# Three block products in place of four at a second level of a Toeplitz convolution, with its tables from difference vectors

## The chip, the cores and the metric

The kernel runs on one core of one Trainium2 chip, as one launch. The metric is device time in microseconds, the median of several executions. Five engines run queues of their own: TensorE (PE, with its weight loads as PEld), VectorE (DVE), ScalarE (ACT), GpSimd (POOL) and SyncE (SP), which here only issues DMAs.

## The reference

For x of 2048 tokens by 1024 channels the result is `x + S4(xn) + FFN(xn)`, with xn the layer norm of x. The part that matters here is S4, a causal convolution along the 1024 channels:

```python
K = _s4_kernel(Lambda, p, q, B, Ct, step, L).astype(u.dtype)     # 1024 taps, made from small vectors
y = jnp.fft.irfft(jnp.fft.rfft(u, n=n) * jnp.fft.rfft(K, n=n), n=n)[..., :L]
return y + D[0] * u
```

The FFN multiplies xn with int4 weights (1024 to 2752, gate and up), forms `silu(g) * u` and multiplies with a third int4 matrix (2752 to 1024).

## The kernel before, in words

All matrix work is on PE. A float32 operand is split in two fp16 parts, high and low, and a product is three matmul passes (`PASS`: high by high, high by low, low by high). Token and channel blocks are combined by Strassen-like sums, so that seven products stand for eight.

There are two phases. In the first, to about 844 us, PE multiplies xn by the gate and up weights, 21 groups (`gate_up`) for each of two token halves `cp`. DVE, ACT and POOL dequantize weights meanwhile, and the S4 kernel vector is worked out in small steps (`s4`) between them. The instructions of DVE, ACT, PE and SP are pinned to the order in which they are written there (`pin`). The last gate-up group writes its result in fp16 parts to a DRAM tensor `HPL`, by DMAs on ACT's queue (`last_h`).

The second phase starts with the convolution, from 846.6 to 966.4 us, and ends with the down projection (`operands`, `matmuls`, `evacuate`): 49 products of 60 matmuls of 256 columns each, whose results are added to `out` through DMAs. In this phase a scheduler that keeps its own cost estimates orders each engine's queue when the kernel is built; SBUF tiles come from rotating pools. A pool's first tiles take memory that tiles of the first phase held, and wait for their last readers. A DMA of SP or ACT adds to one of eight counters in turn when it lands, and waits for the DMA that used the counter before.

The convolution as a matrix is a lower triangular Toeplitz matrix of 8 by 8 blocks of 128 channels. A tile of the stage is 128 tokens (`q`, four of them) of one token quarter (`cp`, `c`) by 512 output channels (`hh`: 0 the left half, 1 the right). There are 32 such tiles.

- `band` holds the Toeplitz rows for lags 0 to 1023 in both fp16 parts. It is read from the vector `KP` in DRAM, which the S4 steps wrote, by four overlapping-row DMAs on SP.
- `conv` multiplies four 128-channel blocks of xn (as weights) with 512, 384, 256 and 128 columns of `band`: the triangle. For `hh = 1` it adds the square part, from the other half's four blocks, as a 2 by 2 product of 256-wide blocks with three products for four: two of them with the tables `diff[0]` and `diff[1]`, 256 columns each, in `conv`, and one with the sums `xs` of input blocks, in `last_tiles`, which goes to a bank of its own (`pc`) and is added to both 256-wide halves of the result.
- `diff` comes from `band` by DVE and ACT (`add_split`), `xs` from xn in the same way, eight blocks of 512 tokens.
- `last_tiles` also adds the remaining 192 channels of the down projection, five 512-column matmuls with `wp` (loaded by two DMA transposes of `WPN`) and `hpl` (loaded from `HPL` on ACT's queue). It then loads a tile of x (`p`), adds the PSUM result to it on DVE and stores it to `out`.
- One quarter of the transposed xn is not kept in SBUF and is loaded from `XSP` for each `cp` (x7; in the trace `x<-XSP`).

The order is (c, hh) = (0,0), (0,1), (1,1), (1,0) in the first half, where `last_tiles` runs four tiles behind `conv`, and (0,1), (0,0), (1,1), (1,0) in the second, where it follows at once and the first four operands of the down projection are prepared (`prepare`: loads `a`, `b`, splits `g`). PSUM has eight banks. In the trace, `cv` is a tile's bank, `cc` the bank `pc`, and L77 and L82 are two lines of the wrapper through which engines are called, with and without a pinned order.

Of the kernel before, what the change touches and what calls it, by code (L numbers as in the profile page):

```python
# [24 lines left out]
F16 = mybir.dt.float16  # L25
# [4 lines left out]
ALU = mybir.AluOpType  # L30
# [3 lines left out]
P = 128  # L34
# [21 lines left out]
KS = 64.0  # L56
# [31 lines left out]
def build(nc, tc, x, xp, raw_d, sz_d, par_d, vct_d, tab_d, csrow_d, out):  # L88
# [3 lines left out]
    with es:  # L92
        pool = lambda name, **k: es.enter_context(tc.tile_pool(name=name, **k))
        dr = pool("dr", bufs=1, space=DRAM)
        cst = pool("cst", bufs=1)
# [18 lines left out]
        V, A = Engine(tc, nc.vector), Engine(tc, nc.scalar)  # L114
        SP, G, PE = Engine(tc, nc.sync), nc.gpsimd, Engine(tc, nc.tensor)
# [7 lines left out]
        ident = cst.tile([P, P], F32, name="ident")  # L123
# [11 lines left out]
        home, szbufs = {"nat": weights("right", "nat", bufs=4)}, [4]  # L135
# [10 lines left out]
        xf = {}  # L146
# [141 lines left out]
        with ea:  # L288
# [273 lines left out]
            PASS = ((0, 0), (0, 1), (1, 0))  # L562
# [177 lines left out]
            sm, wx, cf, tmp = s4p[:, 0:32], s4p[:, 32:36], s4p[:, 36:44], s4p[:, 44:46]  # L740
# [66 lines left out]
            def s4_kernel():  # L807
# [4 lines left out]
                M, AD, SB = ALU.mult, ALU.add, ALU.subtract  # L812
# [40 lines left out]
                tab, z, tab2 = tab[:, 0:512], tab[:, 512:896], tab2[:, 0:272]  # L853
                SP.dma_start(tab, tab_d[0])
                SP.dma_start(tab2[0:8], tab_d[1, 0:8, 0:272])
                yield "bank"
                py = bank("s4y")

# [1 line left out]
                    PE.matmul(py[0:8, 0:256], W(8), tab[:, 0:256], start=True, stop=False)  # L860
                PE.matmul(py[0:8, 0:256], W(9), tab[:, 256:512], start=False, stop=True)
                yield "read"
                tc_, ts_ = tab2[0:8, 0:128], tab2[0:8, 128:256]
                yr, yi = py[0:8, 0:128], py[0:8, 128:256]
                zt = z[0:8, 256:384]
# [7 lines left out]
                pk = bank("s4k")[0:8, 0:128]  # L873
                with tc.issue_after(ends[0].ins):
                    PE.matmul(pk, tab2[0:8, 256:264], z[0:8, 0:128], start=True, stop=False)
                PE.matmul(pk, tab2[0:8, 264:272], z[0:8, 128:256], start=False, stop=True)
                yield "read"
                k = z[:, 256:384]
                V.tensor_copy(k[0:8], pk)
                V.scalar_tensor_tensor(k[0:1, 0:1], sm[0:1, 24:25], KS, k[0:1, 0:1], M, AD)  # L880
                kh = cst.tile([8, 2, P], F16, tag="s4kh", name="s4kh")
                split(kh, k[0:8])
# [303 lines left out]
        for b in range(2):  # L1186
            for n in range(2):
                p0 = 64 * b + 32 * n
                base = KP[:, 128 - 64 * b - 62 - n :]
                src = bass.AP(base.tensor, base.offset, [[2, 32], [base.ap[0][0], 2], [1, 1024]])  # L1190
                SP.dma_start(band[p0 : p0 + 32], src)

        def add_split(dst, srcs, op):

            (h0, l0), (h1, l1) = srcs
            n = dst.shape[2]
            t = htile("t")[:, 0:n]
            V.tensor_tensor(t, h0, h1, op)
            V.tensor_tensor(t, t, l0, ALU.add)
            V.tensor_tensor(t, t, l1, op)  # L1200
            A.copy(dst[:, 0], t)
            V.tensor_tensor(dst[:, 1], t, dst[:, 0], ALU.subtract)


        diff = []
        for a0, b0 in ((128, 384), (640, 384)):
            a, b = ([band[:, i, c : c + 384] for i in range(2)] for c in (a0, b0))
            diff.append(htile(f"diff{a0}").bitcast(F16).rearrange("p (a b) -> p a b", a=2)[:, :, 0:384])
            add_split(diff[-1], (a, b), ALU.subtract)
        wp = []  # L1210
        for i in range(2):
            wp.append(bep.tile([P, 2, 1024], F16, tag="be", name=f"wp{i}"))
            SP.dma_start_transpose(wp[i].rearrange("p b (c d) -> p (b c) d", d=P), WPN[:, i])

        def conv(cp, c, hh, q, xc):

            ts = slice(q * P, (q + 1) * P)
            ps = bank(f"cv{cp}{c}{hh}{q}")
            first = [True]

            def mm(dst, w, m):
                PE.matmul(dst, w, m, start=first[0], stop=False, skip_group_check=True)
                first[0] = False

            xt = xc[2 * c + hh]
            for k in range(4):
                for xi, bi in PASS:
                    mm(ps[:, P * k : 512], xt[:, xi, k, ts], band[:, bi, 0 : 512 - P * k])
            if hh:

                xt = xc[2 * c]
                for k in range(2):
                    for xi, bi in PASS:
                        mm(ps[:, 0:256], xt[:, xi, k + 2, ts], diff[0][:, bi, P - P * k : P - P * k + 256])
# [5 lines left out]
        def last_tiles(ps, cp, c, hh, q, hpl, xs):  # L1240

            ts = slice(q * P, (q + 1) * P)
            cols = slice(512 * hh, 512 * hh + 512)
            mm = lambda w, m, stop=False: PE.matmul(ps, w, m, start=False, stop=stop, skip_group_check=True)
            for hi, wi in PASS:
# [6 lines left out]
            V.scalar_tensor_tensor(o, ps, osc, o, ALU.mult, ALU.add)  # L1252
            if hh:
                pc = bank(f"cc{cp}{c}{q}")
                for k in range(2):
                    for n, (xi, bi) in enumerate(PASS):
                        PE.matmul(pc[:, 0:256], xs[:, c, xi, k, ts], band[:, bi, 512 - P * k : 768 - P * k],
                                  start=(k == 0 and n == 0), stop=(k == 1 and n == 2))
# [13 lines left out]
            if n < len(items):  # L1272
                ready.append(operands(*items[n], n))

        for cp in range(2):
            home, tag = (gp, "g") if cp else (cvp, "cv")
            hpl = home.tile([P, 2, 3, 512], F16, tag=tag, name=f"hpl{cp}")
            A.dma_start(hpl, HPL[cp])
            x7 = fp.tile([P, 2, 4, 512], F16, tag="f", name=f"x7_{cp}")
            SP.dma_start(x7, XSP[cp])  # L1280
            xc = [xf[cp, 3], xf[cp, 1], x7, xf[cp, 0]]
            xs = fp.tile([P, 2, 2, 2, 512], F16, tag="f", name=f"xs{cp}")
            for c in range(2):
                for k in range(2):
                    a, b = ([xc[2 * c][:, i, m, :] for i in range(2)] for m in (k, k + 2))
                    add_split(xs[:, c, :, k, :], (a, b), ALU.add)

            behind = []
            for c, hh in ((0, 0), (0, 1), (1, 1), (1, 0)) if cp == 0 else ((0, 1), (0, 0), (1, 1), (1, 0)):
                for q in range(4):  # L1290
                    behind.append((conv(cp, c, hh, q, xc), cp, c, hh, q))
                    if len(behind) > 4 - 4 * cp:
                        last_tiles(*behind.pop(0), hpl, xs)
                if cp:
                    prepare()
            while behind:
                last_tiles(*behind.pop(0), hpl, xs)


        U = [uxp.tile([P, 4, 512], F32, tag="ux", name=f"U{cp}") for cp in range(2)]  # L1300
# [204 lines left out]
```

## Time and profile before

| What | Value |
|---|---|
| median of 3 executions | 1293.04 us (1291.49 to 1295.91) |
| the profiled execution | 1293.54 us, span 1291.5 us |
| busy in the span: PE, DVE, ACT, POOL | 1258.9, 1007.7, 672.1, 177.4 us |
| matmuls | 7880 |
| matmuls `cv<-band` and `cv<-diff` | 384 and 192, 846.6 to 965.2 us |
| matmuls `cc<-band` | 96 |
| matmuls `cv<-wp` | 160, 128x512, 857.1 to 966.1 us |
| granted PE clock, mean over the span | 0.994 |

A line of the trace's timeline gives the start, the length, the engine, the source line, the operation, `out<-in`, the shape and the count of merged instructions; in brackets, how long the engine was idle before and what released it. A matmul's own duration contains a fixed tail; matmuls that follow each other start closer together than that. A line of windows gives the stretch, its length, and the busy time and number of instructions of PE, PEld, DVE, ACT and POOL, then the granted PE clock, the busy share of the DMA engines and GB/s. A line of DMA issues ends with the KB of each and the median time from issue to landing. SPq and ACTq are the DMA issues of SP and ACT.

### The profile page before, as it was taken

The numbers are of one execution on the slowest core, as the hardware profiler recorded it, in microseconds if no ns is written. First come the engines' busy times: TensorE is split into PE (matmuls) and PEld (weight loads), VectorE is DVE, ScalarE is ACT, GpSimd is POOL, SyncE is SP. The second block draws the span as 40 slices with busy tenths as digits, with TensorE's granted clock in tenths as the row PEclk, the third lists the DMA queues.
The fourth block names the chain that finished last, engine by engine and source line by source line (L and its number), as shares of the span: only waits on it lengthen the run. The fifth ranks groups of instructions, "written<-read, shape, count | busy, mean of one in ns | idle before, by whom it ended". The sixth has DMA issues, their size and how long they took to land. (4 is left out here: it accounts for less than half of the span.)

```text
span 1291.5 us, 20871 instructions
## 1 busy us (share of the span) xinstructions
PE 1258.9 (97%) x7880; PEld 753.2 (58%) x7880; DVE 1007.7 (78%) x1344; ACT 672.1 (52%) x1208; POOL 177.4 (14%) x267
## 2 busy tenths in 40 slices
PE   5999999999999999999998999999999999999998
PEld 5744344444444444444443444456668888888887
DVE  6789974888978788878788887663758898779792
ACT  4868476666657556656666675620105433443330
POOL 2230010200010000100010001000000131356440
PEclk8999999999999999999999999999999999999999
DMA  6692938789795959889998998775938778999981
GB/s 222 147 227 59 203 101 157 213 218 239 162 252 144 253 146 241 224 209 235 244 239 216 260 243 201 226 264 183 350 122 344 239 230 226 256 283 259 288 176 50
DMA packets 358401, 276.04 MB, mean 214 GB/s; under 512 B 211668, under 2 KB 304668, under 8 KB 354204
## 3 DMA queue, kind: packets, MB, share of 16 engines
q1 hardware_dynamic: 335676, 261.59, 74.1%
q0 software_dynamic: 21760, 10.49, 6.9%
q10 hardware_dynamic: 864, 2.62, 0.5%
q8 instruction: 62, 1.02, 0.3%
q14 instruction: 39, 0.32, 0.1%
HBM read 132.36 MB, written 94.84 MB: 176 GB/s over the span
## 5 line engine op out<-in xcount | busy, mean ns | idle before, releaser
L82 PEld LDWEIGHTS <-wf 128*128 128x128 f16 x2807 | 274.0, 98 | 341.0 <-issue 7.0
L77 PEld LDWEIGHTS <-g 128*128 128x128 f16 x2940 | 287.7, 98 | 33.5
L82 ACT ACTIVATE w<-w,sz 128x64 f32<-128x64 int32 x560 | 196.0, 428 | 68.4 <-DVE w L82 51.3
L77 ACT CAST g<-a 128x2560 f16<-128x2560 f32 x42 | 97.5, 2324 | 176.6 <-PE A L77 50.4
L82 PE MATMUL D<-x,wf 128*128 128x512 f16 x816 | 188.0, 380 | 0.9 <-ACT D L82 0.9
L77 PE MATMUL A<-b,g 128*128 128x256 f16 x1680 | 185.9, 273 | 0.0
L82 PE MATMUL A<-x,wf 128*128 128x512 f16 x791 | 177.7, 380 | 5.1 <-DMA wf<-nat 4.7
L82 PE MATMUL C<-x,wf 128*128 128x512 f16 x804 | 179.1, 379 | 0.0
L82 DVE TENSOR_TENSOR w<-w 128x256 f32<-128x256 f32 (+1 forms) x244 | 132.6, 544 | 39.5 <-ACT w L82 32.3
L77 PEld LDWEIGHTS <-wf 128*128 128x128 f16 x1152 | 100.1, 100 | 98.4 <-DMA wf<-nat 4.3
L77 DVE TENSOR_TENSOR g<-a,g 128x2560 f16<-128x2560 f32 x42 | 118.5, 2823 | 29.6 <-ACT g L77 29.6
L1357 POOL DMA_DIRECT2D out<-o x64 | 78.8, 2127 | 320.7 <-DVE o L77 309.8
L82 ACT CAST nd<-w 128x896 f16<-128x896 f32 x70 | 65.2, 932 | 82.8 <-DVE w L82 65.6
L322 POOL TENSOR_SCALAR sz<-sz 128x16 f32<-128x16 f32 x42 | 16.5, 392 | 632.8 <-DMA sz<-in_sz 586.5
L77 PE MATMUL D<-b,g 128*128 128x256 f16 x840 | 94.0, 273 | 0.0
L82 PE MATMUL B<-x,wf 128*128 128x512 f16 x396 | 90.9, 379 | 2.1 <-ACT B L82 2.1
L82 DVE TENSOR_TENSOR nd<-w,nd 128x896 f16<-128x896 f32 x70 | 76.1, 1086 | 9.2 <-ACT nd L82 9.2
L82 ACT CAST nat<-w 128x896 f16<-128x896 f32 x62 | 55.2, 936 | 34.1 <-ACT B L82 17.0
L77 PEld LDWEIGHTS <-x 128*128 128x128 f16 x576 | 53.4, 98 | 25.0 <-issue 1.1
L82 DVE TENSOR_TENSOR nat<-w,nat 128x896 f16<-128x896 f32 x62 | 64.8, 1085 | 1.5 <-ACT nat L82 1.5
L77 PE MATMUL cv<-band,x 128*128 128x512 f16 (+3 forms) x384 | 57.1, 299 | 1.0 <-DVE hb L82 1.0
L77 DVE SCALAR_TENSOR_TENSOR p<-cv,p 128x512 f32<-128x512 f32 x32 | 22.0, 689 | 43.3 <-PE cv L77 33.6
(169 smaller groups left out, 1408.6 us busy)
## 6 DMA issues: line engine op xcount, KB each, us to landing
a<-HF SPq DMA_DIRECT2D x28, 1280.0 KB, 8.0
WD<-nd SPq DMA_DIRECT2D x70, 448.0 KB, 4.1
b<-WD SPq DMA_DIRECT2D x49, 640.0 KB, 6.0
w<-SZT SPq DMA_DIRECT2D x80, 256.0 KB, 5.4
raw<-in_raw SPq DMA_DIRECT2D x65, 256.0 KB, 4.0
HF<-ha SPq DMA_DIRECT2D x54, 256.0 KB, 3.4
HF<-s SPq DMA_DIRECT2D x40, 256.0 KB, 2.8
HF<-hb SPq DMA_DIRECT2D x36, 256.0 KB, 3.6
```

The costliest lines, as they stand in the source:

```text
L77: return method(*args, **kw)
L82: self.last = method(*args, **kw)
L322: G.tensor_scalar(sz[:, 0], sz[:, 0], WS, None, ALU.mult)
L1357: G.dma_start(dst, o[:, q], accum_op=ALU.add)
```

## The change

The triangle's near blocks and one part of the square get a second level of three products for four, at blocks of 128. For `hh = 0` the square of 2 by 2 blocks of 128 below the diagonal (from input blocks 0 and 1 to output columns 256 to 511) leaves `conv`; `crossed` does two of its three products with tables `near`, and the third uses a sum of input blocks with `band`. For `hh = 1` the second half of the square (`diff[1]`, to columns 256 to 511) is done so, with tables `far` and the sum times `fall`. The third product goes to 128 columns of the bank `pc`, which every tile now has, and DVE adds it to both 128-wide halves.

The tables are no longer made from `band`. The S4 steps form more vectors with the DFT rows of the kernel: differences of the rows, on POOL (`rows`, `step`, `less`), so that the same PE product gives 21 rows instead of 8. They go to DRAM as `KP`, `KD` (five) and `KQ` (eight), and twelve overlapping-row DMAs on SP, in place of four, load `band`, `fall` (replacing `diff[0]`) and `parts` (`near`, `far`). SP is pinned for these loads, the wp transposes and the first XSP load. `fall`, `parts` and the second `hpl` share a tile `side` of the pool `g`.

The sums `xs` become three blocks for each token quarter (`block_sums`) where there were two, with the low parts added in fp16, in steps placed between the tiles (`sums_steps`). The order of tiles becomes (0,0), (1,0), (0,1), (1,1) in the first half and (0,0), (0,1), (1,0), (1,1) in the second, and `pc` is multiplied ahead of the wp matmuls.

```diff
+        KD = dr.tile([2, 640], F16, name="KD")
+        KQ = dr.tile([2, 8 * P], F16, name="KQ")
...
+                rows = tab2[0:8, 272:335].rearrange("p (a b) -> p a b", a=3)
+                step = tab2[0:8, 335:356].rearrange("p (a b) -> p a b", a=3)
...
+                less = lambda dst, src, a, b, n=2: G.tensor_tensor(dst, src[:, :, a : a + n], src[:, :, b : b + n], SB)
+                less(step, rows, 0, 1, 7)
+                less(rows[:, :, 8:13], rows, 0, 2, 5)
+                for n, args in enumerate(((rows, 0, 1), (rows, 2, 1), (step, 4, 2), (step, 3, 5))):
+                    less(rows[:, :, 13 + 2 * n : 15 + 2 * n], *args)
...
-                SP.dma_start(KP[:, 128:1152].rearrange("a (b c) -> b a c", b=8), kh)
+                SP.dma_start(KP[:, 128:1152].rearrange("a (b c) -> b a c", b=8), kh[0:8])
+                SP.dma_start(KD.rearrange("a (b c) -> b a c", b=5), kh[8:13])
+                SP.dma_start(KQ.rearrange("a (b c) -> b a c", b=8), kh[13:21])
...
+        SP.pin = True
         band = bep.tile([P, 2, 1024], F16, tag="be", name="band")
...
+        toeplitz(band, KP, [[1280, 2], [1, 1024]])
+        side = gp.tile([P, 5120], F16, tag="g", name="side")
+        fall = side[:, 0:1024].rearrange("p (a b) -> p a b", a=2)
+        toeplitz(fall, KD, [[640, 2], [1, 512]])
+        parts = side[:, 1024:2048].rearrange("p (a b c) -> p a b c", a=2, b=4)
+        toeplitz(parts.rearrange("p a b c -> p (a b) c"), KQ, [[2 * P, 8], [1, P]])
+        near, far = ([parts[:, :, n + i] for i in range(2)] for n in (0, 2))
...
+        def block_sums(dst3, c, xc, sets):
+
+            add = ALU.add
+            for i in sets:
+                a, b = ((0, 1), (0, 2), (1, 3))[i]
...
+                    V.tensor_tensor(t, xt[:, 0, a], xt[:, 0, b], add)
+                A.copy(dst[:, 0], t)
+                V.tensor_tensor(dst[:, 1], t, dst[:, 0], ALU.subtract)
+                V.tensor_tensor(t16, xt[:, 1, a], xt[:, 1, b], add)
+                summed.append(V.tensor_tensor(dst[:, 1], dst[:, 1], t16, add))
+        def crossed(ps, xt, k, col, pair, ts):
+
+            for xi, bi in PASS:
+                for n in range(2):
+                    c0 = col + P * n
+                    PE.matmul(ps[:, c0 : c0 + P], xt[:, xi, k + 1 - n, ts], pair[n][:, bi],
+                              start=False, stop=False, skip_group_check=True)
...
             for k in range(4):
-                for xi, bi in PASS:
-                    mm(ps[:, P * k : 512], xt[:, xi, k, ts], band[:, bi, 0 : 512 - P * k])
+                lo, hi = P * k, 512 if hh else 256 * (k // 2) + 256
+                for n, (xi, bi) in enumerate(PASS):
+                    PE.matmul(ps[:, lo:hi], xt[:, xi, k, ts], band[:, bi, 0 : hi - lo],
+                              start=(k == 0 and n == 0), stop=False, skip_group_check=True)
...
-                for k in range(2):
-                    for xi, bi in PASS:
-                        mm(ps[:, 256:512], xt[:, xi, k, ts], diff[1][:, bi, P - P * k : P - P * k + 256])
+                crossed(ps, xt, 0, 256, far, ts)
...
+            pc = bank(f"cc{cp}{c}{hh}{q}")
...
+            else:
+                crossed(ps, xc[2 * c], 0, 256, near, ts)
+            both = fall[:, :, 384:512] if hh else band[:, :, 256:384]
+            for n, (xi, bi) in enumerate(PASS):
+                PE.matmul(pc[:, 256:384], xs[:, 0, xi, ts], both[:, bi],
+                          start=(not hh and n == 0), stop=(n == 2), skip_group_check=True)
...
+            ov = o[:, 256:512].rearrange("p (a b) -> p a b", a=2)
+            V.scalar_tensor_tensor(
+                ov, pc[:, 256:384].unsqueeze(1).to_broadcast([P, 2, P]), -osc if hh else osc, ov, ALU.mult, ALU.add)
...
-            for c, hh in ((0, 0), (0, 1), (1, 1), (1, 0)) if cp == 0 else ((0, 1), (0, 0), (1, 1), (1, 0)):
+            for c, hh in ((0, 0), (1, 0), (0, 1), (1, 1)) if cp == 0 else ((0, 0), (0, 1), (1, 0), (1, 1)):
```

More of the change, by code (lines that the diff above doesn't have):

```diff
@@ L852, in s4_kernel @@
                 tab, tab2 = (wtemp("nat", [P, 896], F32, f"s4t{i}") for i in range(2))
-                tab, z, tab2 = tab[:, 0:512], tab[:, 512:896], tab2[:, 0:272]
+                tab, z, tab2 = tab[:, 0:512], tab[:, 512:896], tab2[:, 0:512]
                 SP.dma_start(tab, tab_d[0])
-                SP.dma_start(tab2[0:8], tab_d[1, 0:8, 0:272])
+                SP.dma_start(tab2[0:8, 0:272], tab_d[1, 0:8, 0:272])
                 yield "bank"
@@ L862, in s4_kernel @@
                 yield "read"
+                rows = tab2[0:8, 272:335].rearrange("p (a b) -> p a b", a=3)
+                step = tab2[0:8, 335:356].rearrange("p (a b) -> p a b", a=3)
+                one = tab2[0:8, 384:512]
+                G.tensor_copy(rows[:, 0:2, 0:8], tab2[0:8, 256:272].rearrange("p (a b) -> p a b", a=2))
+                G.tensor_copy(rows[:, 2, 0:8], ident[0:8, 0:8])
+                less = lambda dst, src, a, b, n=2: G.tensor_tensor(dst, src[:, :, a : a + n], src[:, :, b : b + n], SB)
[3 more added lines that the diff above has]
+                    less(rows[:, :, 13 + 2 * n : 15 + 2 * n], *args)
+                G.memset(one, 0.0)
+                G.tensor_scalar(one[0:1, 0:1], sm[0:1, 24:25], KS, None, M)
                 tc_, ts_ = tab2[0:8, 0:128], tab2[0:8, 128:256]
@@ L872, in s4_kernel @@
                 yield "bank"
-                pk = bank("s4k")[0:8, 0:128]
+                pk = bank("s4k")[0:21, 0:128]
                 with tc.issue_after(ends[0].ins):
-                    PE.matmul(pk, tab2[0:8, 256:264], z[0:8, 0:128], start=True, stop=False)
-                PE.matmul(pk, tab2[0:8, 264:272], z[0:8, 128:256], start=False, stop=True)
+                    PE.matmul(pk, rows[:, 0], z[0:8, 0:128], start=True, stop=False)
+                PE.matmul(pk, rows[:, 1], z[0:8, 128:256], start=False, stop=False)
+                PE.matmul(pk, rows[:, 2], one, start=False, stop=True)
                 yield "read"
[L878 to L882, printed above, removed]
+                k = z[0:21, 256:384]
+                V.tensor_copy(k, pk)
+                kh = cst.tile([21, 2, P], F16, tag="s4kh", name="s4kh")
+                split(kh, k)
                 yield
@@ L1182, in operands, with toeplitz @@
             return gsplit(src, f"g{k}_{m}"), b
-        band = bep.tile([P, 2, 1024], F16, tag="be", name="band")
[L1186 to L1209, printed above, removed]
+        def toeplitz(dst, rows, inner):
+            for b in range(2):
+                for n in range(2):
+                    p0 = 64 * b + 32 * n
+                    base = rows[:, P - 64 * b - 62 - n :]
+                    src = bass.AP(base.tensor, base.offset, [[2, 32]] + inner)
+                    SP.dma_start(dst[p0 : p0 + 32], src)
+        SP.pin = True
+        band = bep.tile([P, 2, 1024], F16, tag="be", name="band")
+        toeplitz(band, KP, [[1280, 2], [1, 1024]])
[5 more added lines that the diff above has]
+        near, far = ([parts[:, :, n + i] for i in range(2)] for n in (0, 2))
         wp = []
@@ L1213, in build @@
             SP.dma_start_transpose(wp[i].rearrange("p b (c d) -> p (b c) d", d=P), WPN[:, i])
+        summed, emptied = [], []
+        def block_sums(dst3, c, xc, sets):
+            add = ALU.add
+            for i in sets:
+                a, b = ((0, 1), (0, 2), (1, 3))[i]
+                xt, dst, t = xc[2 * c], dst3[:, i], htile("t")
+                t16 = t.bitcast(F16)[:, 0:512]
+                with ExitStack() as order:
+                    for done in (summed[-2:-1], emptied[-1:]):
+                        for op in done:
+                            order.enter_context(tc.issue_after(op.ins))
+                    V.tensor_tensor(t, xt[:, 0, a], xt[:, 0, b], add)
[5 more added lines that the diff above has]
+            for xi, bi in PASS:
+                for n in range(2):
+                    c0 = col + P * n
+                    PE.matmul(ps[:, c0 : c0 + P], xt[:, xi, k + 1 - n, ts], pair[n][:, bi],
+                              start=False, stop=False, skip_group_check=True)
         def conv(cp, c, hh, q, xc):
@@ L1218, in conv @@
             ps = bank(f"cv{cp}{c}{hh}{q}")
[L1219 to L1223, printed above, removed]
             xt = xc[2 * c + hh]
             for k in range(4):
-                for xi, bi in PASS:
-                    mm(ps[:, P * k : 512], xt[:, xi, k, ts], band[:, bi, 0 : 512 - P * k])
+                lo, hi = P * k, 512 if hh else 256 * (k // 2) + 256
+                for n, (xi, bi) in enumerate(PASS):
+                    PE.matmul(ps[:, lo:hi], xt[:, xi, k, ts], band[:, bi, 0 : hi - lo],
+                              start=(k == 0 and n == 0), stop=False, skip_group_check=True)
             if hh:
@@ L1233, in conv, with last_tiles @@
                     for xi, bi in PASS:
-                        mm(ps[:, 0:256], xt[:, xi, k + 2, ts], diff[0][:, bi, P - P * k : P - P * k + 256])
-                for k in range(2):
-                    for xi, bi in PASS:
-                        mm(ps[:, 256:512], xt[:, xi, k, ts], diff[1][:, bi, P - P * k : P - P * k + 256])
+                        PE.matmul(ps[:, 0:256], xt[:, xi, k + 2, ts], fall[:, bi, P - P * k : P - P * k + 256],
+                                  start=False, stop=False, skip_group_check=True)
+                crossed(ps, xt, 0, 256, far, ts)
             return ps
-        def last_tiles(ps, cp, c, hh, q, hpl, xs):
+        def last_tiles(ps, cp, c, hh, q, hpl, xc, xs):
             ts = slice(q * P, (q + 1) * P)
@@ L1244, in last_tiles @@
             mm = lambda w, m, stop=False: PE.matmul(ps, w, m, start=False, stop=stop, skip_group_check=True)
+            pc = bank(f"cc{cp}{c}{hh}{q}")
+            if hh:
+                for k in range(2):
+                    for n, (xi, bi) in enumerate(PASS):
+                        PE.matmul(pc[:, 0:256], xs[:, 1 + k, xi, ts], band[:, bi, 512 - P * k : 768 - P * k],
+                                  start=(k == 0 and n == 0), stop=False, skip_group_check=True)
+            else:
+                crossed(ps, xc[2 * c], 0, 256, near, ts)
+            both = fall[:, :, 384:512] if hh else band[:, :, 256:384]
+            for n, (xi, bi) in enumerate(PASS):
+                PE.matmul(pc[:, 256:384], xs[:, 0, xi, ts], both[:, bi],
+                          start=(not hh and n == 0), stop=(n == 2), skip_group_check=True)
             for hi, wi in PASS:
@@ L1251, in last_tiles @@
             SP.dma_start(o, x[t0 : t0 + P, cols])
-            V.scalar_tensor_tensor(o, ps, osc, o, ALU.mult, ALU.add)
+            emptied.append(V.scalar_tensor_tensor(o, ps, osc, o, ALU.mult, ALU.add))
             if hh:
[L1254 to L1258, printed above, removed]
                 ov = o.rearrange("p (a b) -> p a b", a=2)
@@ L1273, in prepare, with sums_tile, lower_parts @@
                 ready.append(operands(*items[n], n))
[L1275 to L1278, printed above, removed]
+        xcs, xss = [None, None], {}
+        def sums_tile(cp, c):
+            xss[cp, c] = fp.tile([P, 3, 2, 512], F16, tag="f", name=f"xs{cp}{c}")
+        def lower_parts(cp):
             x7 = fp.tile([P, 2, 4, 512], F16, tag="f", name=f"x7_{cp}")
@@ L1280, in build, with sums_steps @@
             SP.dma_start(x7, XSP[cp])
[L1281 to L1286, printed above, removed]
+            xcs[cp] = [xf[cp, 3], xf[cp, 1], x7, xf[cp, 0]]
+        def sums_steps():
+            first, rest = (0,), (1, 2)
+            for cp in range(2):
+                for c, sets in ((0, first), (1, first), (0, rest), (1, rest)) if cp == 0 else (
+                        (0, first), (0, rest), (1, first), (1, rest)):
+                    if (cp, c) not in xss:
+                        sums_tile(cp, c)
+                    if xcs[cp] is None:
+                        with tc.issue_after(emptied[0].ins):
+                            lower_parts(cp)
+                    for i in sets:
+                        block_sums(xss[cp, c], c, xcs[cp], (i,))
+                        yield
@@ L1288, in build, with finish @@
+        lower_parts(0)
+        SP.pin = False
+        summing = sums_steps()
+        for cp in range(2):
+            hpl = side[:, 2048:5120].rearrange("p (a b c) -> p a b c", a=2, b=3) if cp else cvp.tile(
+                [P, 2, 3, 512], F16, tag="cv", name="hpl0")
+            A.dma_start(hpl, HPL[cp])
+            xc = xcs[cp]
             behind = []
-            for c, hh in ((0, 0), (0, 1), (1, 1), (1, 0)) if cp == 0 else ((0, 1), (0, 0), (1, 1), (1, 0)):
+            def finish():
+                b = behind.pop(0)
+                last_tiles(*b, hpl, xc, xss[cp, b[2]])
+            for c, hh in ((0, 0), (1, 0), (0, 1), (1, 1)) if cp == 0 else ((0, 0), (0, 1), (1, 0), (1, 1)):
@@ L1290, in build @@
                 for q in range(4):
                     behind.append((conv(cp, c, hh, q, xc), cp, c, hh, q))
+                    if (c, hh) == (0, 0) or q % 2:
+                        next(summing, 0)
                     if len(behind) > 4 - 4 * cp:
-                        last_tiles(*behind.pop(0), hpl, xs)
+                        finish()
                 if cp:
@@ L1296, in build @@
             while behind:
-                last_tiles(*behind.pop(0), hpl, xs)
+                if len(behind) % 2:
+                    next(summing, 0)
+                finish()
         U = [uxp.tile([P, 4, 512], F32, tag="ux", name=f"U{cp}") for cp in range(2)]
```

## The prediction

> **What bounds the kernel now.** First the page: engine shares and the slices.
>
> ```profile
> PE 1258.9 (97%) x7880; PEld 753.2 (58%) x7880; DVE 1007.7 (78%) x1344; ACT 672.1 (52%) x1208; POOL 177.4 (14%) x267
> PE   5999999999999999999998999999999999999998
> ```
>
> TensorE works 97% of the span. Next the windows of the convolution stage (846.6 to 966.4 us) and of the products behind it:
>
> ```profile
> 846.60:849.40 2.80, 1.79 (x13) 1.09 (x12) 1.38 (x2) 0.89 (x3) 0.00 (x0) 1.00 0.54 130
> 849.40:857.10 7.70, 7.44 (x55) 4.77 (x54) 6.79 (x13) 1.62 (x3) 0.00 (x0) 1.00 0.95 344
> 857.10:900.00 42.90, 42.89 (x308) 28.88 (x309) 19.35 (x31) 2.44 (x4) 0.00 (x0) 1.00 0.62 203
> 966.40:1291.50 325.10, 321.06 (x2941) 287.52 (x2939) 256.17 (x171) 117.76 (x63) 98.40 (x80) 1.00 0.84 236
> ```
>
> The second number is PE's busy time. PE is idle for about 1 us near 848 and 0.3 us near 857, then hardly at all to the end. So each microsecond of PE work taken from this stage comes off the end, and each new PE wait is added to it. The timeline of PE gives the price of a column:
>
> ```profile
> 31.38 0.83 PE L77 MATMUL g<-x,wf 128*128 128x128 f16 x12
> 32.05 0.83 PE L77 MATMUL u<-x,wf 128*128 128x128 f16 x12
> 846.60 1.79 PE L77 MATMUL cv<-band,x 128*128 128x512 f16 x12
> 849.40 6.68 PE L77 MATMUL cv<-band,x 128*128 128x512 f16 x48 [1.01 <-DVE hb L82]
> 857.11 1.25 PE L77 MATMUL cv<-wp,hpl 128*128 128x512 f16 x5 [0.27 <-DMA hpl<-HPL]
> ```
>
> Forty-eight matmuls with 15,360 columns take 6.68 us less the tail of the last (0.22 us, the 128-wide duration): 0.424 ns a column. Twelve 128-wide ones start in 32.05-31.38 = 0.67 us, 56 ns each, weights reloaded every time. Last, SP's queue, the DMAs that ACT issues, and times to landing:
>
> ```profile
> 830.83 3.00 SPq L77 DMA_DIRECT2D band<-KP  x4
> 833.87 4.84 SPq L77 DMA_TRANSPOSE wp<-WPN  x2
> 838.81 0.53 SPq L77 DMA_DIRECT2D x<-XSP  x1
> 847.18 10.70 SPq L77 DMA_DIRECT2D p<-in_x  x4
> ```
>
> ```profile
> 840.88 0.33 ACTq L82 DMA_DIRECT2D HPL<-hpl  x1
> 847.64 0.36 ACTq L82 DMA_DIRECT2D HPL<-hpl  x1
> 850.76 0.33 ACTq L82 DMA_DIRECT2D HPL<-hpl  x1
> 851.20 0.37 ACTq L77 DMA_DIRECT2D hpl<-HPL  x1
> 853.71 0.33 ACTq L77 DMA_DIRECT2D hpl<-HPL  x1
> ```
>
> ```profile
> x<-XSP SPq DMA_DIRECT2D x2, 1024.0 KB, 6.8
> hpl<-HPL ACTq DMA_DIRECT2D x2, 768.0 KB, 5.9
> band<-KP SPq DMA_DIRECT2D x4, 128.0 KB, 2.9
> wp<-WPN SPq DMA_TRANSPOSE x2, 4.6
> ```
>
> Today every table of the stage is under way by 839, eight microseconds before PE wants the first.
>
> **PE work.** Each of the 32 tiles loses 384 columns (three products of 128 for four, three passes): 12,288 x 0.424 = 5.2 us. But the 16 left tiles get 9 more matmuls and the 16 right ones 3 more, 192 in all; a 128-wide one costs 56 ns where 128 columns at the wide rate cost 54, so about 2.4 ns each, 0.45 us. Net gain 4.75 us. This is the change's purpose, and it is real: nothing in the 56 ns row says that weight loading slows narrow matmuls.
>
> A rule speaks against that last sentence. The Trainium skill, "TensorE: Matmul & The Clock Gate", section "Back-to-back issue gap", gives about 81 ns for a 128-wide matmul in a stream of weight loads. By it the 336 additional 128-wide matmuls would cost 25 ns more each, 8.4 us, and turn the gain into a loss of 3.7. I use the 56 ns row.
>
> **The tables.** The old code made both difference tables from the band on DVE and ACT (852 to 857.5). The new code loads them: four DMAs each from KD and KQ, issued on SP between the band and the wp transposes. Two things hold them, both legible in the instruction lists of the built kernels. The tile they land in (`side`) takes memory of the last gate-up's output pieces, so the first KD load waits until the second HPL write has landed: 840.88 + 4.5 = 845.4. And every DMA of SP and ACT counts on one of eight completion counters in turn, and waits for the counter's previous DMA. The four KQ loads get the counters of four DMAs of ACT's queue, listed above: the HPL writes of 847.64 and 850.76, and the hpl loads of 851.20 and 853.71. The fourth KQ load can thus not start before the hpl load of 853.71 is in: 853.7 + 5.9 = 859.6; with band's 2.9 it lands at 862.5. PE's fifth step, the crossed near product, waits for all four.
>
> PE gets there early. The first tile (2,304 columns, 0.98 us) ends at 847.6, then the bank wait to 849.4 stays, since its releaser (hb) has not moved: that wait grows by 0.64 to 1.8 us. Three more tiles end at 852.3. **Wait 1: 862.5-852.3 = 10.2 us.** Its bounds: a 768 KB load between the 640 KB b load at 847 (4.3 us) and 5.9, the KQ load itself between the 2.5 of a WPN write and the 3.7 of a p load: 8.2 to 11.0.
>
> Behind KQ stand, on SP in order, the wp transposes, the XSP load, b, the second XSP load and the p loads. Wp starts at 860.0 and lands at 864.6, while PE ends its 24 crossed matmuls (1.3 us) at 863.9: **wait 2, 0.7 us**. Then 20 wp matmuls of 0.215 end at 868.9. SP is busy 4.84 us with the transposes, so XSP goes at 864.9 and lands after 6.0 (the 1,280 KB load at 900) to 6.8 (its own row), at 871.2: **wait 3, 2.4 us** (1.5 to 3). The old order wanted XSP's part at the ninth tile, the new one wants it at the fifth, so nothing hides it.
>
> The clock: after idle stretches of 2.6 and 1.3 us near 690 the window 692-696 has a granted clock of 0.58, and three matmuls there took 1.46 us for 0.82. The gap of 10 us should bring that at least once, 1.7 us of lost work in 3.4. I count nothing, since it ends before 871 and XSP's wait covers it; without that cover it costs 1.7 to 3.4.
>
> The same page's section "Part 1: The HAM clock gate" says the clock halves after an idle window of about 3.4 us. The row shows the halving after two shorter gaps. By the rule the cost is one or two such windows, mostly under wait 3.
>
> **DVE.** Block sums: 12 sets of two f32 steps (0.69) and two all-f16 steps (half of the 128x1024 f16 row's 0.688: 0.35), 25 us, for the old 32 x 0.69 + 8 x 0.55 = 26.5. Evacuations: the same 48 of 0.69 plus 32 of 128x256 (0.42): +13.4. DVE is about 70 us busy in the stage's 120, so 82 does not bound; the order does. The instruction list has two places. After XSP lands, ten sum steps (4.8 us) stand ahead of the first evacuation, while PE has two tiles, 5.1 us less the pipeline: **wait 4, 0.7 (0 to 2)**. At the second half's start DVE holds, in order, g_1 (2.82), two evacuations, a sum, g_2 (2.82), and only then the second evacuations that free the banks PE wants; g_1 itself waits for ACT's 2.32 copy of an operand whose load was pushed back with the SP queue. From reaching g_1 to the needed bank is 2 x 2.82 + 4 x 0.6 + up to 2.4 = 8 to 10.4, against two tiles of 2.55: **wait 5, 5 (2.5 to 6.5)**. Before, the same g steps ran at 911 with banks to spare. At the products' start the third operand's loads wait for the last tiles: **wait 6, 0.5 (0 to 2)**.
>
> The POOL steps added for the vectors (eleven of 0.4 to 1.2 us) and two more small SP issues sit near 550-570, about 25 us ahead of their reader. They cost nothing; without that cover up to 10 us of POOL time.
>
> **Sum.** New PE idle 1.8+10.2+0.7+2.4+0.7+5+0.5 = 21.3; old 1.6 (the rows' 1.01 and 0.27, each with the 0.17 us tail of a matmul); work -4.75. Total +15.0. On the profiled execution, 1293.54 (span 1291.5 and 2.0 around it), that is 1308.5; it lies 0.5 above the median, so 1308.
>
> **Rivals.** *The tables come in time* (ends faster): if the KQ counters were free by 849.4, as band's are today by 837, waits 1 to 3 vanish and the stage is PE-bound: -4.75 + 0.64 for the first bank wait, -0.4 for the gap near 857, and DVE's waits cost 0 to 4: -4.5 to -0.5, 1288.5 to 1292.5. For: PE-bound slices, and three matmuls for four. Against: the ACT queue rows, none of which the change moves earlier. Chance 0.07. It decides if the fourth KQ load starts before 849.4.
> *Only the SP hold* (mine without wait 5): DVE catches up because the a loads land as fast as 6.0 at 900: about 1303. Chance 0.22, in the range.
> *A knock-on*: half clock uncovered (up to 3.4), p loads and b loads bunched behind XSP as the 12 us landings at 907-911, product operands late by some us: 1314 to 1322. Chance 0.16, half of it in the range.
> My own case has 0.55. Low end: the lower bounds of all waits, 1.8+8.2+0.5+1.5+0+2.5+0 = 14.5, gives 1301. High: 1316. A measurement of this kernel can tell about 0.3% (3.9 us) from no change; the first rival lies on both sides of that: faster 0.04, same 0.03, slower 0.93.
>
> **What would show it.** Right: a PE gap of about 10 us at stage offset 5.8, ended by a DMA into `side`; SP's wp rows near 860 instead of 834, XSP near 865; half clock in a window near 865; PE gaps of a few us released by DVE p around 925; products as long as before. Wrong: `side` loads issued before 850, 128-wide cv matmuls at 80 ns, or DVE gaps all through the second half.

## The result and the profile after

The changed kernel takes 1306.72 us (median of 6 runs, 1304.73 to 1309.59) where the kernel before, run beside it, takes 1293.23: a ratio of 1.0102, with a 95% interval of 1.0081 to 1.0122. The profiled execution took 1307.03 us, its span 1305.1. Of the 13.5 us between the two profiled executions, 13.2 lie in the convolution stage (first to last `cv` matmul: 119.5 before, 132.7 after), 0.3 ahead of it, in a first phase that ended later, and 0.1 behind it.

First the page, engine shares and slices:

```profile
PE 1257.7 (96%) x8074; PEld 759.8 (58%) x8074; DVE 1019.8 (78%) x1383; ACT 673.6 (52%) x1210; POOL 184.0 (14%) x277
PE   6999999999999999999998999969899999999998
```

PE is 1.2 us less busy, in a span that is 13.7 longer: less work, more idle time, in slices 27 and 29. The windows of the stage show how much of it:

```profile
846.94:849.70 2.76, 1.15 (x13) 0.96 (x12) 1.38 (x2) 0.88 (x3) 0.00 (x0) 1.00 0.25 95
849.70:852.90 3.20, 3.13 (x36) 2.75 (x35) 1.29 (x2) 0.61 (x1) 0.00 (x0) 1.00 0.49 124
852.90:861.47 8.57, 0.01 (x1) 0.04 (x2) 1.54 (x3) 0.62 (x1) 0.00 (x0) 0.80 0.63 204
861.47:865.75 4.28, 2.71 (x24) 2.55 (x25) 0.00 (x0) 0.00 (x0) 0.00 (x0) 0.61 0.98 162
865.75:870.20 4.45, 4.45 (x21) 1.92 (x21) 0.02 (x1) 0.00 (x0) 0.00 (x0) 1.00 1.11 386
870.20:900.00 29.80, 28.76 (x276) 21.40 (x276) 23.71 (x49) 4.93 (x8) 0.00 (x0) 1.00 0.74 253
900.00:930.00 30.00, 25.69 (x220) 17.77 (x218) 23.73 (x37) 6.51 (x5) 0.00 (x0) 1.00 0.80 295
930.00:979.85 49.85, 49.85 (x441) 35.75 (x440) 23.49 (x40) 0.00 (x0) 0.00 (x0) 1.00 0.53 178
```

Column two is PE's busy time, column eight the clock. Four tiles in, PE stands still for 8.6 us. Then it works at a clock of 0.61, with another pause, and 4.3 us are idle between 900 and 930. From 930 it is never idle. The timeline of PE and the DMA issues of SP name what ended the first pauses:

```profile
861.47 2.72 PE L77 MATMUL cv<-side,x 128*128 128x128 f16 x24 [8.62 <-DMA side<-KQ]
865.75 4.48 PE L77 MATMUL cv<-wp,hpl 128*128 128x512 f16 x20 [1.57 <-DMA wp<-WPN]
```

```profile
843.29 1.71 SPq L82 DMA_DIRECT2D side<-KD  x4
850.01 9.58 SPq L82 DMA_DIRECT2D side<-KQ  x4
859.63 4.03 SPq L82 DMA_TRANSPOSE wp<-WPN  x2
863.78 1.60 SPq L82 DMA_DIRECT2D x<-XSP  x1
```

The four KQ issues are spread over 9.58 us. What SP waited for in 840 to 870 (us in total, times, longest):

```profile
SPq L82 <- DMA HPL<-hpl: 15.4, 3, 7.5
SPq L82 <- DMA side<-HPL: 2.8, 1, 2.8
SPq L82 <- DMA hpl<-HPL: 2.5, 1, 2.5
```

Every one is a DMA of ACT's queue, none of them data that KQ needs. For the gaps near 921 and 925 the timeline of DVE shows what stood ahead of the evacuations (`p<-cv,p` and `p<-cc,p`, which add a bank to a tile of x and so free the bank): the splits `g<-a,g`, which make the low part of an operand of the down projection.

```profile
918.70 2.83 DVE L77 TENSOR_TENSOR g<-a,g 128x2560 f16<-128x2560 f32 x1 [1.87 <-ACT g L77]
921.44 1.28 DVE L77 SCALAR_TENSOR_TENSOR p<-cv,p 128x512 f32<-128x512 f32 x2
922.64 0.68 DVE L77 TENSOR_TENSOR t<-x 128x512 f32<-128x512 f16 x1
923.24 2.82 DVE L77 TENSOR_TENSOR g<-a,g 128x2560 f16<-128x2560 f32 x1
925.98 1.28 DVE L77 SCALAR_TENSOR_TENSOR p<-cc,p 128x512 f32<-128x512 f32 x2
```

To compare kernels, PE's idle time is taken below from start to start of neighbouring matmuls, less the pitch of the first (the distance to the next start when nothing waits): so 8.8 for the pause of 8.62, and 1.2 and 0.4 for the two old ones.

### The profile page after: what moved, and what is told of

Its sections match the earlier page's. It is cut to its first block, busy times and chain, and to the rows that moved or that the text cites. A ratio compares the mean times of both kernels' runs of the same rounds, so it can differ in the third digit from the quotient of the medians.

```text
span 1305.1 us, 21317 instructions
## 1 busy us (share of the span) xinstructions
PE 1257.7 (96%) x8074; PEld 759.8 (58%) x8074; DVE 1019.8 (78%) x1383; ACT 673.6 (52%) x1210; POOL 184.0 (14%) x277
## 5 line engine op out<-in xcount | busy, mean ns | idle before, releaser
L77 PE MATMUL cv<-band,x 128*128 128x128 f16 (+3 forms) x384 | 46.8, 272 | 7.0 <-DVE p L77 5.3
L77 PE MATMUL g<-x,wf 128*128 128x128 f16 (+1 forms) x336 | 49.3, 295 | 1.8 <-ACT wf L82 0.8
```

The source lines that it names most:

```text
L77: return method(*args, **kw)
```

## The experiments

The theory on record: PE really has 4.75 us less to do, and it is lost by two separate causes, the hold of SP's queue at the stage's start and DVE's order near the second half's start. The rivals were that the narrow matmuls give nothing back, and that all waits are one chain. The table holds all kernels; the last three columns are from one profile each. Time lost at half clock is what the stage takes beyond its waits and PE's work, which is 117.9 us in the kernel before and 113.3 in those with the change (from e7, e8 and e9, which have no half clock there).

| Kernel | us | ratio to before | stage | PE's waits in it, in order | lost at half clock |
|---|---|---|---|---|---|
| before | 1293.2 | 1 | 119.5 | 1.2 bank, 0.4 hpl | 0 |
| changed | 1306.7 | 1.0102 (1.0081 to 1.0122) | 132.7 | 1.8 bank, 8.8 KQ, 1.8 wp, 0.1 XSP, 1.2 DVE, 1.1 + 3.5 DVE | 1.1 |
| e1 | 1301.2 | 1.0064 (1.0048 to 1.0080) | 128.3 | 1.8 bank, 5.9 KQ, 1.0 + 3.6 DVE | 2.8 |
| e2 | 1303.7 | 1.0088 (1.0074 to 1.0102) | 133.1 | 1.8 bank, 9.3 KQ, 2.7 wp, 3.2 p | 2.9 |
| e3 | 1300.5 | 1.0047 (1.0030 to 1.0064) | 129.5 | 1.8 bank, 7.4 KQ, 3.2 p | 3.8 |
| e4 | 1302.6 | 1.0071 (1.0058 to 1.0084) | 131.0 | 1.8 bank, 7.5 KQ, 0.9 + 3.5 DVE | 4.0 |
| e5 | 1299.6 | 1.0047 (1.0030 to 1.0064) | 128.5 | 1.8 bank, 2.2 KQ, 3.1 hpl, 0.7 + 3.6 DVE | 3.8 |
| e6 | 1300.2 | 1.0055 (1.0039 to 1.0070) | 129.2 | 1.8 bank, 9.2 KQ, 1.9 wp, 0.6 DVE | 2.5 |
| e7 | 1289.1 | 0.9966 (0.9954 to 0.9979) | 117.1 | 1.8 bank, 2.0 hpl | 0 |
| e8 | 1287.1 | 0.9954 (0.9941 to 0.9967) | 116.4 | 1.8 bank, 1.3 hpl | 0 |
| e9 | 1293.2 | 1.0014 (1.0003 to 1.0025) | 121.0 | 1.8 bank, 1.5 hpl, 0.9 + 3.5 DVE | 0 |

A ratio is to the runs of the kernel before that were taken beside the kernel, with medians of 1291.8 to 1293.2. The profiled execution isn't always near the median: it took 1298.4 us in e1, 1301.4 in e5, 1289.0 in e8 and 1291.0 in e9.

**e1: the table loads on POOL's queue.**

```diff
-        def toeplitz(dst, rows, inner):
+        def toeplitz(dst, rows, inner, queue=SP):
...
-                    SP.dma_start(dst[p0 : p0 + 32], src)
+                    queue.dma_start(dst[p0 : p0 + 32], src)
...
-        toeplitz(fall, KD, [[640, 2], [1, 512]])
+        toeplitz(fall, KD, [[640, 2], [1, 512]], G)
...
-        toeplitz(parts.rearrange("p a b c -> p (a b) c"), KQ, [[2 * P, 8], [1, P]])
+        toeplitz(parts.rearrange("p a b c -> p (a b) c"), KQ, [[2 * P, 8], [1, P]], G)
```

> The changed kernel, but the eight loads of KD and KQ into side are issued on POOL's DMA queue instead of SP's; nothing else is edited. Against the changed kernel's 1306.7 us. My theory (the waits at the stage's start come from SP's queue and from ACT's loads whose counters the KQ loads wait for; the later wait on DVE is a cause of its own): the wp transposes and the first XSP load go back to about 834 to 840, the KQ loads start when the HPL write of 840.9 has landed (about 845) and land by 852. Gone are wait 1 (8.8), wait 2 (1.8), XSP's 0.1, the 1.4 lost at half clock and the first DVE wait (1.2), 13.3 in all; new is a wait of 2 to 3.4 for hpl, whose load lands at 857 while PE wants it at 853.7. The wait on DVE near the second half's start, 4.6, stays. 1295 to 1297.5. Rival A (all new waits are one chain, and the DVE wait of the second half comes from the late loads too): it goes as well, 1290 to 1292. Rival B (PE would have been held anyhow, by DVE or hpl): the waits move elsewhere, 1302 to 1306.

Measured 1301.2, between the theory and rival B. SP's order came back as foreseen (wp at 829.5, XSP at 833.9), and the waits for wp and XSP and the first one on DVE are gone. But KQ was still late. POOL issued its loads from 846.7 to 849.0, and PE got them at 856.7:

```profile
856.66 0.80 PE L77 MATMUL cv<-side,x 128*128 128x128 f16 x6 [5.69 <-DMA side<-KQ]
```

```profile
x<-XSP SPq DMA_DIRECT2D x2, 1024.0 KB, 8.5
side<-KQ POOLq DMA_DIRECT2D x4, 64.0 KB, 8.1
```

The second row, of the DMA issues, has 8.1 us from issue to landing, against 2.2 for the KD loads in the changed kernel, whose last KQ load was also followed by PE 2.2 after its issue. So the hold on SP was one reason why the tables were late, but without it they still landed late: an hpl load, an HPL write and p loads were now under way together with KQ. The second XSP load wasn't: it had landed at 843.0, before POOL issued the first table load at 844.3. The two gaps of the second half stayed, against rival A, and 2.8 us went at half clock, where the theory had none left.

**e2: DVE's splits behind the evacuations.**

```diff
-            V.tensor_tensor(g[:, :, 1], src, g[:, :, 0], ALU.subtract)
+            with tc.issue_after(emptied[-1].ins) if name in late else nullcontext():
+                V.tensor_tensor(g[:, :, 1], src, g[:, :, 0], ALU.subtract)
```

`late` names the first four operands; `issue_after` orders an instruction behind another when the kernel is built.

> The changed kernel, but DVE's splits of the first four operands of the down projection (g) are ordered behind the evacuations of the tiles written ahead of them; the loads stay on SP. My theory (the gaps of 1.1 and 3.5 us near 921 and 925 are evacuations that stand behind two splits of 2.8 us): both gaps go, waits 1 to 4 stay: 1306.7 - 4.6 = 1302, 1301 to 1303.5. Rival A (DVE is behind on all its work there, so whatever stands ahead of the evacuations): the gap stays in another place, 1305 to 1308. Rival B (the operands come too late for the products): 1 to 3 us of new waits at 980, 1303 to 1306.

Measured 1303.7, 0.2 above the theory's upper edge and with an interval that overlaps that of the changed kernel, so the time alone decides little. It lies in rival B's range too, but the products behind the stage wait no longer than in the changed kernel (0.3). The gap of 1.1 went, but that of 3.5 only became 3.2, with another releaser: DVE now waits for a load of x.

```profile
926.53 1.34 DVE L77 SCALAR_TENSOR_TENSOR p<-cv,p 128x512 f32<-128x512 f32 x2 [3.30 <-DMA p<-in_x]
```

Two things were late at that place, and the second showed when the first was gone.

**e3: e1 and e2 together.**

> Both edits in one kernel: the KD and KQ loads on POOL's queue, and DVE's splits behind the evacuations. My theory (two causes that add, and a true saving of 4.9 us of PE work beneath them): the sum of the two effects, 1306.7 - 10.5 - 4.6 = 1291.6, 1290 to 1293, so 0 to 3 below the kernel before; what is left over the saving is the first bank wait (1.8 for 1.2) and the wait for hpl (2 to 3.4 for 0.3). Rival A (the narrow matmuls give nothing back, PE work unchanged or more): 1296 or more. Rival B (one chain): no more than the larger of the two effects, 1295 to 1297.

Measured 1300.5, within the bounds that rival A had set. It still does not show rival A, since the waits are there to be seen: 7.4 for KQ (8.5 from issue to landing), 3.2 for p, and two stretches at half clock. The theory's sum failed because neither edit had removed the main wait that it was aimed at, and half clock cost 3.8.

**e4: wp and XSP ahead of KD and KQ on SP** (the lines of the two wp transposes and of `lower_parts(0)` moved up behind the band's).

> The changed kernel, but on SP the two wp transposes and the first XSP load stand ahead of the KD and KQ loads. All loads stay on SP. My theory (wait 1 is the KQ loads' own hold, by the memory of side and by the counters of ACT's HPL writes and loads; only waits 2 and 3 and the DVE wait behind them come from the order on SP): wait 1 stays at 8 to 10, the other three (1.8, 0.1, 1.2) go: 1302.5 to 1305. Rival (the KQ loads are late because of what stands ahead of them on SP, so putting more ahead makes them later): wait 1 grows by the 5.4 us of the transposes and the XSP issue, 1307 to 1310.

Measured 1302.6, as the theory had it. SP issues wp at 831.2 and XSP at 836.0, and the KQ loads at 850.8 to 858.4 although wp and XSP are out of SP's way before 840. The last goes 13.6 us into the stage; in two profiles of the changed kernel it was 12.3 and 13.4. So their hold is their own, and wp and XSP were only behind it. The wait for KQ is 7.5, below the 8 to 10 of the theory, because PE had work until 8.3 us into the stage, not 5.9; the three waits behind it are gone, and half clock cost 4.0.

**e5: e1, with the second XSP load behind the p loads on SP.**

```diff
-            SP.dma_start(o, x[t0 : t0 + P, cols])
+            taken.append(SP.dma_start(o, x[t0 : t0 + P, cols]))
...
-                        with tc.issue_after(emptied[0].ins):
+                        with tc.issue_after(taken[-1].ins):
```

> The kernel with the KD and KQ loads on POOL's queue (1301.2 us, PE's wait for KQ 5.9, KQ 8.5 from issue to landing), and the second XSP load is moved behind the p loads on SP: there it was issued at 834.5, right behind the first, and in the changed kernel itself at 865.9. My theory (KQ lands late there because the second megabyte of XSP, b, p and hpl are under way at the same time; alone it took 2.2): KQ lands 3 to 5 after its issue, the wait for it falls to 1 to 2.5, the wait for hpl then shows with 1 to 2, and the half clock behind it (1.0) goes: 1297 to 1299.5. Rival (loads on POOL's queue land late by themselves, whatever else is under way): 1300 to 1302.

(The 8.5 in that text is e3's row; e1's own is 8.1.) Measured 1299.6, between the two. KQ landed 6.5 after its issue, not 3 to 5; the wait for it fell to 2.2, as said, but the wait for hpl came out at 3.1 and the half clock stayed. The theory's reason doesn't hold either: in e1 the second XSP load had landed 3.6 us before the first KQ load was issued. What the move did change is the start of the table loads, 0.3 us ahead of the stage in place of 1.6 into it; by which wait stays open.

In no run did KQ come on POOL's queue without other loads (4.1 to 8.5). But e4 has KQ on SP's queue with loads of hpl beside it: its four loads took 7.5, 4.8, 4.7 and, when hpl had landed, 2.0 us. So traffic alone can make the tables that late; whether POOL's queue adds to it stays open.

**e6: e2, with the a loads of the first product behind the p loads on SP.**

```diff
-            SP.dma_start(t, HF[r][PROD[k][0], :, half * c : half * c + half, :])
+            with tc.issue_after(taken[-1].ins) if k == 1 else nullcontext():
+                SP.dma_start(t, HF[r][PROD[k][0], :, half * c : half * c + half, :])
```

> The kernel with DVE's splits behind the evacuations (1303.7 us, one gap of 3.24 left at 923.8, where DVE waits for a p load), and the a loads of the first product are ordered behind the p loads on SP. My theory (a's third load waits for the last read of the first half's sums and x7, which hold all six buffers of its pool, and the p loads stand behind it on SP): the gap of 3.24 goes: 1300 to 1301.5. Rival A (the p loads are late for want of buffers or by their own 5 us): 1303 to 1304.5. Rival B (the a loads become too late for the products): new waits at 980 to 1000, 1302 to 1306.

Measured 1300.2, as the theory had it; no gap is left in the second half, and the products wait no longer than in the changed kernel (0.3). So the p loads stood behind a's third load on SP. That this one waited for the buffers which the new sums take is read from the instruction list; no run shows it by itself, and the edit of the a loads alone was not tried.

**e7: all of it**, with KQ first and both tables in tiles of their own:

```diff
-        side = gp.tile([P, 5120], F16, tag="g", name="side")
-        fall = side[:, 0:1024].rearrange("p (a b) -> p a b", a=2)
+        fall = htile("fall").bitcast(F16).rearrange("p (a b) -> p a b", a=2)
+        parts = htile("parts").bitcast(F16).rearrange("p (a b c) -> p a b c", a=2, b=4)
+        toeplitz(parts.rearrange("p a b c -> p (a b) c"), KQ, [[2 * P, 8], [1, P]], G)
+        toeplitz(fall, KD, [[640, 2], [1, 512]], G)
```

> The edits together: KQ's and KD's loads on POOL's queue, KQ first and both into tiles of their own (free about 3 us before side is), the second XSP load and the a loads behind the p loads, DVE's splits behind the evacuations. My theory (every wait that was found is a cause by itself, PE's work is 4.9 less): left are the first bank wait of 1.8 and 2 to 4 for hpl; a stage of 113 + 1.8 + 3 = 118 against 119.5 before: 1290.5 to 1294. Rival A (the three-for-four products save PE nothing): 1297 or more. Rival B (DVE or the DMA engines are simply full there, and each wait taken away comes back at the next place): 1297 to 1301, with a gap of over 3 somewhere.

**e8: e7, with the first hpl load on POOL's queue** (`G.dma_start(hpls[0], HPL[0])` behind the table loads).

> The same, and the first hpl load is issued on POOL's queue behind the table loads, about where ACT issued it or a little earlier, which also lets the scheduler place more of the crossed and summed products ahead of the first wp products. My theory (the wait for hpl can be filled with other tiles' work): 1 to 2.5 less than without it: 1289 to 1292.5. Rival (the load lands as late as KQ did on that queue, 8 us after issue): 1293 to 1297.

Measured 1289.1 and 1287.1, both faster than the kernel before, by 0.3% and 0.5%, and both below the theories' ranges, by 1.4 and 1.9. Part of that isn't in the stage, which is 117.1 for the theory's 118 in e7; and of the 2.0 between e7 and e8 the stage holds 0.8. PE's timeline of e7 has one gap left after the first bank wait; in e8 the scheduler put 36 crossed products ahead of the first wp products, and the gap is shorter:

```profile
854.31 1.25 PE L77 MATMUL cv<-wp,hpl 128*128 128x512 f16 x5 [1.83 <-DMA hpl<-HPL]
```

```profile
853.20 2.17 PE L77 MATMUL cv<-parts,x 128*128 128x128 f16 x36
856.47 6.22 PE L77 MATMUL cv<-wp,hpl 128*128 128x512 f16 x28 [1.10 <-DMA hpl<-HPL]
```

**e9: e7 without the edits of the second half.**

> The kernel of all edits (1289.1 us) without the two of the second half: KQ and KD on POOL's queue, KQ first, in tiles of their own, the second XSP load behind the p loads; DVE's splits and the a loads as in the changed kernel. My theory (the two places are independent causes): the start of the stage looks as in the kernel of all edits, with 1.8 for the first bank and about 2 for hpl, and the gaps near the second half's start are there with 4 to 4.7: 1289.1 + 4.4 = 1293.5, 1292 to 1295, which is the kernel before's time within 0.2%. Rival (the second half's gaps were an echo of the late start, as the two gaps of 0.7 and 3.6 that stayed in the earlier runs could be, since those starts were late too): they go with it, 1289 to 1290.5.

Measured 1293.2, the ratio 1.0014: the theory's number. The start of the stage is repaired and the gaps near the second half's start are all there, 0.9 and 3.5. They were no echo of the late start, and the two edits of the second half together are worth 3.9 us of the stage.

**Further profiles of the kernels before and after.** The stages of e7 and e8 are only 2.4 and 3.2 us shorter than before's, their times 3.8 and 5.8.

> The kernel before, unchanged, for a second profile. The question: the two best kernels are 3.8 and 5.8 below it by their medians, but their convolution stage is only 2.4 and 3.2 shorter in the profiles. My theory: the first phase, which no edit of these experiments touches, ends at a time that differs from execution to execution by some 3 us (842.7 to 846.9 in ten profiles), and the one profile of before (846.6) lies at the late end; here the stage starts between 842.5 and 846, its length stays 119.5 within 0.5, and the products behind it 321. Rival: the change makes the first phase shorter by 2; the stage starts at 846 to 847.5 again.

> The same kernel again, a third profile, with the same question: start of the stage between 842.5 and 846 by my theory, 846 to 847.5 by the rival; the stage's length 119.5 within 0.5.

> The changed kernel, unchanged, for a second profile. Its stage began at 846.9 in the first and was 132.7 long. By my theory the start moves within 842.5 to 847 as in the others, and the length stays 131 to 134 with the same waits (8 to 10 for KQ, 1 to 3 for wp, about 4.6 on DVE near 921). Rival: the KQ wait depends on when the counters' DMAs land and varies by more than 2.

The stage of the kernel before began at 843.6 and 848.7, its length was 119.8 and 119.6; times 1290.7 and 1295.7. The second start lies above both ranges. So the end of the first phase moves by 5 us between executions, and times of single executions must not be set against each other; stage lengths may. The changed kernel's began at 844.2, with 9.8 for KQ and 1.8 for wp, within the ranges said, and was 134.3 long (1305.9), 0.3 above its range, since half clock cost 2.9 in place of 1.1. Whether the first phase of the changed kernels also ends a little earlier as a rule (844.3 in the mean of 11 profiles, 846.3 in the three of before) stays open; it would be the 2 us by which most of the times lie below what their stage lengths give.

## Why the prediction was right

The forecast was 1308, the time 1306.7. The path was right: less PE work, lost to late tables at the stage's start and to late evacuations near the second half's. Some terms inside it were wrong and made up for each other. Its steps, one by one:

- **PE work, -4.75: measured -4.6.** The stage less all PE waits is 117.9 us in each of the three profiles of before, and 113.3 in e7, e8 and e9. The price of a narrow matmul was right too: e8's 36 of them run 2.17 us less the tail of 0.22, which is 1.95 over 35 starts, 56 ns each. By the Trainium skill's 81 ns ("TensorE: Matmul & The Clock Gate", section "Back-to-back issue gap") PE would have lost; the runs contradict it for this stream. The sum's 0.424 ns a column already holds part of each matmul's fixed cost: from 56 ns for 128 columns and 215 for 512 a column is 0.414, and a matmul's fixed part 3 ns, which gives 4.5.
- **First bank wait, 1.8:** 1.8 in every kernel.
- **Wait 1, 10.2: measured 8.8 and 9.8.** The mechanism held, in e4 and in SP's own waits, down to the fourth load, issued at 859.3 for a forecast of 859.6. The terms mis-sized are KQ's landing, 2.2 for the assumed 2.9 (the DMA engines were 23% busy from 859.3 to 861.5), and the time at which PE gets there, 852.8 for 852.3. The other hold showed too: the first KD load was issued at 843.3, when the second HPL write had landed, which took 2.0 us and not 4.5.
- **Wait 2 (0.7), wait 3 (2.4), half clock (0): measured 1.8, 0.1 and 1.1.** Here a step failed: "XSP's wait covers it". PE did the crossed products at half clock, in 2.6 us for 1.3; wp was waited for longer all the same, since it took 5.9 us to land and not 4.6; and XSP, landed at 870.1, was there when PE wanted it. The three together are 3.0 for 3.1, since the landing of XSP, not the split before it, sets the end of this stretch. In the second profile half clock cost 2.9, so the cover did not hold there.
- **Wait 4, 0.7: 1.2,** and none in the second profile.
- **Wait 5, 5: 4.6.** The size was right and so was the place, but the reason was half of it. Behind the two splits on DVE (1.1 and part of the rest) stood a p load that SP held back (e2, e6). And the step "whose load was pushed back with the SP queue" is wrong: in e9 SP isn't held at the stage's start, the a loads are issued 15.3 us ahead of the long gap, as in the changed kernel (15.6), and the gaps are the same.
- **Wait 6, 0.5: 0.3.**

New idle time and half clock 19.7 (forecast 21.3), old idle time 1.6, PE work -4.6: +13.5. The profiled executions differ by 13.5 too, but that holds the 0.3 of the first phase, so the last tenths of the agreement are luck.

The rival *the tables come in time* can now be priced: e9 is close to that kernel (it also moves the second XSP load), 1293.2 against the 1288.5 to 1292.5 given. It had the gap near 857 going away. In fact PE reaches the first wp products earlier and waits 1.5 to 2 for hpl there. *Only the SP hold* fell with the gaps near 921.

## What to carry to other kernels

Work taken from a busy engine was worth nothing here while a new input of that engine arrived late. When a change replaces a table computed on chip by a loaded one, look for what the load itself must wait for (the last use of its memory, the DMA whose counter it takes over) and what stands behind it on its queue. And when a wait is taken away, look at the same place again: three times here a second cause, nearly as late, stood behind the first (e1, e2, e5), and only the two kernels with all of them repaired showed the saving that the change was made for.

## What the runs showed of the hardware

Two things were not expected. A PE pause of the same length can cost a half clock or nothing. Each trace has the granted clock in stretches of 3.41 us or multiples of it (but for the last, behind PE's work), whose edges lie on one grid for the execution. These are windows of e4 and then of e9, cut at their grids; each has the same pause of 3.33 us (e4 from 919.1 to 922.4, e9 from 908.8 to 912.1):

```profile
919.41:922.82 3.41, 0.39 (x4) 0.36 (x5) 3.41 (x7) 0.00 (x0) 0.00 (x0) 1.00 0.99 371
922.82:926.24 3.42, 3.42 (x24) 2.38 (x22) 3.28 (x7) 0.00 (x0) 0.00 (x0) 0.50 1.05 395
```

```profile
907.13:910.55 3.42, 1.63 (x15) 0.78 (x12) 3.42 (x4) 0.62 (x1) 0.00 (x0) 1.00 1.00 405
910.55:913.96 3.41, 1.87 (x21) 1.56 (x22) 3.41 (x8) 0.00 (x0) 0.00 (x0) 1.00 1.05 399
913.96:917.37 3.41, 3.41 (x34) 2.37 (x32) 3.38 (x8) 0.00 (x0) 0.00 (x0) 1.00 0.77 265
```

In e4 nearly all of the pause falls into one stretch, in which PE works 0.39 us, and the next stretch has half clock: 24 matmuls start in it where 34 start in e9's full one. In e9 an edge divides the pause, PE works 1.63 and 1.87 us in the two stretches, and the clock stays. It comes out the same in all 14 traces: from 20 us on they have some 5,100 such stretches at full clock, and half clock followed those 28 in which PE was busy for at most 0.40 of the time, and none of the others, which begin at 0.41. Of eight pauses of 3.2 to 3.6 us near this place four were followed by it. The Trainium skill ("TensorE: Matmul & The Clock Gate", section "Part 1: The HAM clock gate") has the clock set by a window of about 3.4 us that runs freely; length and free running agree, but the windows ahead of these half clocks weren't all idle: PE was busy for up to 0.40 of them. Where the grid falls differs from execution to execution, so the cost, up to 1.7 us for a stretch full of work, is a matter of chance, and belongs in the range and not in the sum.

And loads of 64 KB took about 2.2 us each on SP's queue with little else under way (KD in the changed kernel), but 4.1 to 8.5 (medians of KQ) on POOL's with megabytes beside them, and 7.5 to 4.7 on SP's too while hpl was loading (e4). That is one reason why e1, alone, gave back half of what it should.
